# A gated graph layer whose loop gets a written order: logits in turn with sums, a fused product ahead of it, the next layer's weights in steps

## The chip, the cores and the metric

The kernel runs on one core of one Trainium2 chip. A core has engines that each run their own instruction stream: TensorE (matmuls into PSUM[...]; PE in the profile, its weight loads PEld), VectorE (DVE), ScalarE (ACT), GpSimd (POOL) and SyncE (SP), which here only issues DMAs. They wait for each other on semaphores. The metric is the device time of one execution in microseconds, and lower is better. Before the change the median of three runs is 1995.79 us (1994.71 to 1996.02).

## The reference

Four graph layers follow each other on a matrix x of 2708 nodes by 128 features, with one dense weighted adjacency matrix adj of 2708 by 2708; each layer's output is added to x, and x is normalised (`x = layernorm(x + layer(x, adj))`). The change is in the second one, called layer 1:

```
messages = x @ W_msg + b_msg
q = messages @ W_q;  k = messages @ W_k
probs = sigmoid(q @ k.T / sqrt(128) + gate_bias)
gates = probs * adj * adj                    # the prior is adj again
aggregated = gates @ messages
updated = relu(concatenate([x, aggregated]) @ W_upd + b_upd)
x = layernorm(x + layernorm(updated) * gamma + beta)
```

Layer 0 computes messages with a gelu for every pair of neighbours. Layer 2 is a layer in hyperbolic space; it has a weight W, a bias b and two attention vectors, and b needs some arithmetic of its own before use (its norm, a tanh, its products with the attention vectors). Layer 3 multiplies adj with x twice. All is f32.

## The kernel before

The 2708 nodes are 22 row tiles of 128, the last with 20 rows. x lies in SBUF for the whole kernel, one tile per 128 columns. The layers run one after the other in one program. The function `layers_1_to_3` (L959) begins with layer 1.

Its first stage goes over groups of up to four tiles: x is transposed (into xT), multiplied with W_msg (mT, the messages with features on partitions), then with the product of W_q and the transpose of W_k (qT), so that a logit is a product of qT and mT; `sums` (L258) makes the messages in rows (mrow) from xT and W_msg, one product of 128 columns per tile. A GpSimd addition (xb, L1003) prepares x plus beta.

The loop (L1012) goes over the 22 tiles of k. A tile of the transposed adjacency (2708 columns, 1354 KB) comes from HBM through SyncE's queue, with three buffers. The 2708 columns are five PSUM banks of 512 and one of 148. For each bank TensorE makes the logits (L1024) into one of two PSUM buffers called lg, and ScalarE puts their sigmoid into w (L1025). VectorE multiplies the whole row of w with the adjacency twice (L1027 and L1028, 128x2708 each); then six products (L1030) add it up, with mrow as weights, in one PSUM tile acc of six banks, over all 22 tiles. There are two w buffers. After the loop VectorE copies acc to aggT (L1032).

The update (L1041) then makes two products per tile, of xT with the upper half of W_upd and of aggT with the lower, adds the bias on VectorE, applies relu on ScalarE and takes the moments of every tile (`moments`, L197). `Resnorm` (L220) normalises twice in two halves of the tiles: `add` for both halves (normalise, times gamma, plus xb, new moments), then `end` for both.

The class `Weights2` (L290) prepares layer 2's weights: it loads W into w2 and the three vectors both as rows spread over all partitions (vecs, by GpSimd's queue, L299) and as columns (SyncE's queue), makes a transpose of W, the arithmetic on the bias, and three columns beside W. It is called at tiles 5, 11 and 16.

What sets the order: in this layer no order is written; a scheduler puts the instructions of each engine in a sequence by what it expects of their times and dependences. It does not have to keep the order of the program: it moved Weights2's loads and its first arithmetic to the very start of the layer, and layer 2's first adjacency loads (L1224) to its start, too. In layers 0 and 3, and in part of layer 2, the order is written: inside `tc.manual_schedule()` each engine runs its instructions as the program lists them.

Of the kernel before, what the change touches and what calls it, by code (L numbers as in the profile page):

```python
# [39 lines left out]
def gnn_stack(ctx: ExitStack, tc: tile.TileContext, t, out: bass.AP):  # L40
# [50 lines left out]
    def over_tiles(r, n=NT, p=P):  # L91
        return r[:p, None, :].to_broadcast([p, n, r.shape[1]])
# [8 lines left out]
    class Values:  # L101


        def __init__(self, pool, tag):
            self.pool, self.tag, self.n = pool, tag, 0
# [155 lines left out]
    def sums(dst, a, b, r, terms, psum, bias):  # L261

        ps = psum.tile([P, BANK // D, D], F32, name="ps")
        for i in range(a, b):
            for k, (src, w) in enumerate(terms):
                nc.tensor.matmul(ps[:r, i - a, :], src[:, i * P:i * P + r], w,  # L266
                                 start=k == 0, stop=k == len(terms) - 1)
        nc.vector.tensor_tensor(dst, ps[:r, :b - a, :], over_tiles(bias, b - a, r), op=ALU.add)  # L268
# [18 lines left out]
    y = const.tile([P, D], F32, name="y")  # L287
    yw = const.tile([P, 3], F32, name="yw")

    class Weights2:  # L290
        def __init__(self, pool):
            self.pool = pool

        def load(self):
            nc.sync.dma_start(out=w2[:, :D], in_=t["L2_WT"])
            self.vecs = self.pool.tile([P, 3, D], F32, name="y2_vecs")
            self.cols = self.pool.tile([P, 3], F32, name="y2_cols")
            for k, name in enumerate(("L2_gnn_b", "L2_gnn_att_wl", "L2_gnn_att_wr")):
                nc.gpsimd.dma_start(out=self.vecs[:, k, :], in_=t[name].partition_broadcast(P))  # L299
                nc.sync.dma_start(out=self.cols[:, k:k + 1], in_=t[name].rearrange("(p o) -> p o", o=1))  # L300
            self.w_rows = self.pool.tile([P, D], F32, name="y2_w_rows")
            self.prods = self.pool.tile([P, 3, D], F32, name="y2_prods")

        def products_with(self, dst, v):
            nc.vector.tensor_tensor(self.prods, self.vecs, v[:, None, :].to_broadcast([P, 3, D]), op=ALU.mult)
            nc.vector.tensor_reduce(dst, self.prods, AX.X, ALU.add)

        def turn(self, ps):
            nc.tensor.transpose(ps[:, :D], w2[:, :D], ident)
            nc.vector.tensor_copy(self.w_rows, ps[:, :D])  # L310

        def bias_point(self):
            V = Values(self.pool, "y2_")
            vecs, cols = self.vecs, self.cols
            sums3 = self.pool.tile([P, 3], F32, name="y2_sums")
            self.products_with(sums3, vecs[:, 0, :])
            bn = V.norm(sums3[:, 0:1])
            bth = V.act(bn, AF.Tanh)
            bk = V.mul(V.mul(bth, V.recip(bn)), V.shrink(bth))
            nc.vector.tensor_scalar(y, vecs[:, 0, :], bk, None, op0=ALU.mult)  # L320
            nc.vector.tensor_copy(vecs[:, 0, :], y)
            nc.vector.tensor_tensor(cols[:, 0:1], cols[:, 0:1], bk, op=ALU.mult)
            self.products_with(yw, y)

        def columns(self, ps):
            nc.tensor.matmul(ps[:, :3], self.w_rows, self.cols, start=True, stop=True)
            nc.vector.tensor_copy(w2[:, D:], ps[:, :3])

# [628 lines left out]
    def layers_1_to_3(top):  # L959

        with ExitStack() as l1:
# [3 lines left out]
            qT = wp.tile([P, N], F32, name="qT")  # L965
            mT = wp.tile([P, N], F32, name="mT")
            aggT = wp.tile([P, N], F32, name="aggT")
            mrow = wp.tile([P, NT, D], F32, name="mrow")
            xb = wp.tile([P, NT, D], F32, name="xb")
            w_msg, w_q, w_k = weight("L1_gnn_W_msg"), weight("L1_gnn_W_q"), weight("L1_gnn_W_k")  # L970
            upd_x, upd_a = weight("L1_gnn_W_upd", 0), weight("L1_gnn_W_upd", P)
# [3 lines left out]

            with ExitStack() as pre:
                psum = pre.enter_context(tc.tile_pool(name="ps_pre1", bufs=2, space=PSUM))

                wT = []
                for w in (w_q, w_k):  # L980
                    ps = psum.tile([P, BANK], F32, name="ps")
                    nc.tensor.transpose(ps[:, :P], w, ident)
                    wT.append(wp.tile([P, P], F32, name=f"wT{len(wT)}"))
                    nc.vector.tensor_copy(wT[-1], ps[:, :P])
                w_qk = wp.tile([P, P], F32, name="w_qk")
                ps = psum.tile([P, BANK], F32, name="ps")
                nc.tensor.matmul(ps[:, :P], wT[0], wT[1], start=True, stop=True)
                nc.vector.tensor_copy(w_qk, ps[:, :P])
                for a, b, r in groups():
                    c = slice(a * P, (b - 1) * P + r)  # L990
                    n = c.stop - c.start
                    ps = psum.tile([P, BANK], F32, name="ps")
                    for i in range(a, b):
                        nc.tensor.transpose(ps[:, (i - a) * P:(i - a) * P + r], x[:r, i, :], ident[:r, :r])
                    nc.scalar.copy(xT[:, c], ps[:, :n])
                    ps = psum.tile([P, BANK], F32, name="ps_m")
                    nc.tensor.matmul(ps[:, :n], w_msg, xT[:, c], start=True, stop=True)
                    nc.scalar.activation(mT[:, c], ps[:, :n], AF.Identity, bias=msg_bc)
                    ps = psum.tile([P, BANK], F32, name="ps_q")
                    nc.tensor.matmul(ps[:, :n], w_qk, mT[:, c], start=True, stop=True)  # L1000
                    nc.vector.tensor_copy(qT[:, c], ps[:, :n])
                    sums(mrow[:r, a:b, :], a, b, r, [(xT, w_msg)], psum, msg_br)
                nc.gpsimd.tensor_tensor(xb, x, over_tiles(beta), op=ALU.add)  # L1003

            with ExitStack() as att:
                gp = att.enter_context(tc.tile_pool(name="gates", bufs=2))
                pacc = att.enter_context(tc.tile_pool(name="ps_agg1", bufs=1, space=PSUM))
                plog = att.enter_context(tc.tile_pool(name="ps_log", bufs=2, space=PSUM))
                acc = pacc.tile([P, N], F32, name="acc")
                weights2 = Weights2(wp)  # L1010
                for j, r in enumerate(rows):
                    at = stream.tile([P, N], F32, name="at")  # L1012
                    nc.sync.dma_start(out=at[:r, :], in_=adjT[j * P:j * P + r, :])
                    if j == NT // 4:
                        weights2.load()
                    elif j == NT // 2:
                        weights2.turn(plog.tile([P, BANK], F32, name="lg"))
                        weights2.bias_point()
                    elif j == NT * 3 // 4:
                        weights2.columns(plog.tile([P, BANK], F32, name="lg"))  # L1020
                    w = gp.tile([P, N], F32, name="w")
                    for a, b in spans(0, N, BANK):
                        lg = plog.tile([P, BANK], F32, name="lg")
                        nc.tensor.matmul(lg[:r, :b - a], mT[:, j * P:j * P + r], qT[:, a:b], start=True, stop=True)  # L1024
                        nc.scalar.activation(w[:r, a:b], lg[:r, :b - a], AF.Sigmoid, bias=gate_b[:r, :],  # L1025
                                             scale=1.0 / math.sqrt(D))
                    nc.vector.tensor_mul(w[:r, :], w[:r, :], at[:r, :])  # L1027
                    nc.vector.tensor_mul(w[:r, :], w[:r, :], at[:r, :])  # L1028
                    for a, b in spans(0, N, BANK):
                        nc.tensor.matmul(acc[:, a:b], mrow[:r, j, :], w[:r, a:b], start=j == 0, stop=j == NT - 1)  # L1030
                for a, b in spans(0, N, BANK):
                    nc.vector.tensor_copy(aggT[:, a:b], acc[:, a:b])  # L1032

            with ExitStack() as upd:
                rp = upd.enter_context(tc.tile_pool(name="upd1", bufs=1))
                psum = upd.enter_context(tc.tile_pool(name="ps_upd1", bufs=4, space=PSUM))
                V = Values(rp, "v1_")
                h = rp.tile([P, NT, D], F32, name="h")
                st = rp.tile([P, NT, 6], F32, name="st")
                nc.vector.memset(h[:, NT - 1, :], 0.0)  # L1040
                for a, b, r in groups():  # L1041
                    g = h[:r, a:b, :]
                    sums(g, a, b, r, [(xT, upd_x), (aggT, upd_a)], psum, upd_b)
                    nc.scalar.activation(g, g, AF.Relu)
                    moments(st, h, a, b)
                Resnorm(h, xb, gamma, st, rp.tile([P, NT, 6], F32, name="st2"), V, xsq).all()

# [584 lines left out]
```

## Time and profile before

| | |
|---|---|
| median of 3 runs | 1995.79 us |
| the profiled execution, and its span | 1993.64 us, 1991.8 us |
| mean granted TensorE clock | 0.92 |
| busy shares TensorE, VectorE, ScalarE, GpSimd | 84%, 77%, 55%, 34% |
| layer 0 | up to about 931.7 us |
| layer 1, first stage | 931.9 to about 970 |
| layer 1, loop up to its last sum | to 1196.4 |
| copies and update, up to the last moment | to 1214.4 |
| both normalisations | to 1239.8 |
| layer 2, layer 3 | to the end |

The profile is one execution; its times are microseconds from the start of its span. "Busy" is the time in which an engine works on an instruction. A line of a timeline names the start, the duration, the engine, the program's line, the operation, what it writes and reads, and how often it ran there; in brackets stands how long the engine was idle before it, and what ended this. The clock is TensorE's: 1.00 is the full one. The shares of the whole span are means over stages with different limits, so the change has to be read from the stretch between 931.9 and about 1246.

### The profile page before, as it was taken

What the parts mean: (1) busy time and instruction counts of PE and PEld (TensorE: products, weight loads), DVE (VectorE), ACT (ScalarE), POOL (GpSimd) and SP (SyncE); (2) the same over time, 40 slices, a digit from 0 to 9 for tenths busy, and PEclk for the clock granted to TensorE, in tenths of its full rate; (3) what the DMA queues carried; (4) which work ended last, traced back from release to release, by engine and by line L of the source; (5) the groups of instructions that cost most, each with busy time, mean ns of one, the idle gap of its engine ahead of it and who ended that gap; (6) DMA issues with size and microseconds to landing.
All of it is one profiled execution on the core that took longest, in us unless ns stands there. A gap on an engine that the chain in (4) does not pass through costs nothing. (4 is left out here: it accounts for less than half of the span.)

```text
span 1991.8 us, 36394 instructions
## 1 busy us (share of the span) xinstructions
PE 1663.9 (84%) x14037; PEld 949.8 (48%) x14037; DVE 1526.7 (77%) x3500; ACT 1103.2 (55%) x1519; POOL 679.0 (34%) x429
## 2 busy tenths in 40 slices
PE   5899999999999999871999994689898983089995
PEld 4666666666666666550444334322232321044542
DVE  7899999999999999876564658699999997810105
ACT  3666676666666666542433323599998983300103
POOL 5677677677577677461000000021000350000000
PEclk9899999999999999995999996779998986589998
DMA  8666666666666676432243310022222217034330
GB/s 224 150 130 135 138 139 128 136 141 127 136 148 122 136 147 111 82 66 88 114 141 139 127 45 1 1 87 88 75 81 95 81 42 293 0 144 167 112 116 30
DMA packets 218359, 222.25 MB, mean 112 GB/s; under 512 B 28373, under 2 KB 204475, under 8 KB 211715
## 3 DMA queue, kind: packets, MB, share of 16 engines
q1 hardware_dynamic: 167038, 195.95, 32.4%
q0 software_dynamic: 51136, 23.88, 10.3%
q8 instruction: 112, 1.84, 0.4%
q14 instruction: 73, 0.59, 0.1%
HBM read 211.94 MB, written 7.83 MB: 110 GB/s over the span
## 5 line engine op out<-in xcount | busy, mean ns | idle before, releaser
L722 POOL DMA_INDIRECT far<-d_tab,ix x352 | 561.8, 1596 | 259.2 <-DVE W L823 112.8
L836 ACT ACTIVATE g<-sl 128x768 f32<-128x768 f32 x484 | 393.4, 813 | 257.9 <-PE sl L763 238.1
L758 PE MATMUL sl<-dA,S 124*128 124x153 f16 x4840 | 408.8, 232 | 10.3 <-DVE W L823 7.8
L758 PEld LDWEIGHTS <-S 124*128 124x128 f16 x4840 | 331.1, 98 | 80.2 <-issue 68.4
L774 PE MATMUL acc<-g,W 128*32 128x128 f32 x4840 | 206.0, 278 | 0.5 <-DVE W L823 0.5
L1227 POOL TENSOR_TENSOR at<-at,off 128x128 f32<-128x128 f32 (+1 forms) x22 | 70.3, 3213 | 336.0 <-DVE m L1256 171.4
L1543 PE MATMUL acc<-held,x 128*128 128x512 f32 (+1 forms) x240 | 99.5, 563 | 84.1 <-DVE x L218 84.1
L774 PEld LDWEIGHTS acc<-g,W 128*32 128x32 f32 x4840 | 140.9, 109 | 58.6 <-issue 54.6
L763 PE MATMUL sl<-s,same 50*128 50x384 f16 x968 | 162.0, 308 | 0.0
L268 DVE TENSOR_TENSOR g<-ps,row_L_gnn_b 128x512 f32<-128x512 f32 (+2 forms) x14 | 7.9, 573 | 197.0 <-PE ps L266 196.9
L1025 ACT ACTIVATE w<-lg,row_L_gnn_gate_bias 128x512 f32<-128x512 f32 (+1 forms) x132 | 80.8, 635 | 137.7 <-PE lg L1024 74.3
L1283 PE MATMUL accV<-m,X 128*128 128x512 f32 (+4 forms) x264 | 128.4, 628 | 33.6 <-DVE m L1273 29.2
L823 DVE TENSOR_TENSOR W<-sl,own 128x150 f32<-128x150 f32 x484 | 143.3, 300 | 14.3 <-ACT g L836 13.6
L1235 PE MATMUL ps<-XT 128*128 128x512 f32 (+4 forms) x264 | 143.2, 626 | 3.1 <-ACT m L1240 2.8
L648 DVE TENSOR_SCALAR S<-rk 124x1000 f16<-124x1000 bf16 (+1 forms) x330 | 134.0, 431 | 0.0
L718 DVE FIND_INDEX8 ix<-v,o 128x8 uint32<-128x2728 f32 x44 | 131.7, 2994 | 0.0
L1024 PE MATMUL lg<-qT,mT 128*128 128x512 f32 (+2 forms) x264 | 115.6, 567 | 18.6 <-ACT w L1025 9.9
L1027 DVE TENSOR_TENSOR w<-w,at 128x2708 f32<-128x2708 f32 (+1 forms) x22 | 65.5, 2975 | 79.3 <-ACT w L1025 79.3
L736 DVE SCALAR_TENSOR_TENSOR extra<-far,v,extra 128x128 f32<-128x128 f32 x330 | 115.0, 349 | 6.3
L1543 PE MATMUL acc<-at,x 128*128 128x512 f32 (+3 forms) x288 | 116.8, 552 | 0.0
L680 DVE SCALAR_TENSOR_TENSOR o<-ps,ar 128x496 f32<-128x496 f32 x132 | 82.4, 624 | 37.3 <-PE ps L669 30.0
L1502 ACT COPY nT<-acc 128x512 f32<-128x512 f32 (+1 forms) x12 | 6.4, 531 | 186.5 <-PE acc L1543 186.5
(319 smaller groups left out, 2675.7 us busy)
## 6 DMA issues: line engine op xcount, KB each, us to landing
at<-in_adjT SPq DMA_DIRECT2D x40, 1354.0 KB
ar<-in_adj SPq DMA_DIRECT2D x105, 248.0 KB
far<-s_tab SPq DMA_DIRECT2D x44, 512.0 KB
at<-in_adjT SPq DMA_DIRECT2D x42, 448.0 KB
at<-in_adjT SPq DMA_DIRECT2D x21, 704.0 KB
at<-in_adjT SPq DMA_DIRECT2D x21, 650.0 KB
held<-in_adjT SPq DMA_DIRECT2D x10, 1354.0 KB
at<-in_adjT SPq DMA_DIRECT2D x21, 280.0 KB
```

The costliest lines, as they stand in the source:

```text
L648: nc.vector.tensor_scalar(self.S[h][:, :n, :, k * RG:(k + 1) * RG], self.rk[h][:, :n, :LR].rearrange("p b (c i) -> p b c i", c=NC), EDGE + ...
L718: nc.vector.max_index(ix, self.v[:, n * 8:n * 8 + 8], self.o.rearrange("p b j -> p (b j)"))
L722: nc.gpsimd.indirect_dma_start(out=self.far[n][:, k, :], out_offset=None, in_=d_tab[:, :], in_offset=bass.IndirectOffsetOnAxis(ap=self.ix[ ...
L758: nc.tensor.matmul(group[c], self.S[h][:, n, c, :], dA[q][:, b, c, :], start=c % 3 == 0 and q == 0, stop=False)
L763: nc.tensor.matmul(out, same[p], self.s3[p, :e - a, :], start=False, stop=True)
L774: nc.tensor.matmul(self.acc[q:q + 32, k, :], W[:, c, :], g[:, c, :], start=b == 0 and k == 0, stop=ends)
L823: nc.vector.tensor_tensor(W[:, :, :RG].rearrange("p (k c) i -> p k c i", k=2), columns_of(sl, D, DA), own[:, None, None, :].to_broadcast([ ...
L836: nc.scalar.activation(g.rearrange("p (k c) d -> p k c d", k=2), columns_of(sl, 0, D), AF.Gelu, scale=1.0 / D_SCALE)
L1024: nc.tensor.matmul(lg[:r, :b - a], mT[:, j * P:j * P + r], qT[:, a:b], start=True, stop=True)
L1235: nc.tensor.matmul(ps, XT[:, self.js], XT[:, c], start=True, stop=False)
L1283: nc.tensor.matmul(accV[:, a:b], X[:self.r, self.j, :], self.m[:, a:b], start=first, stop=last)
L1543: nc.tensor.matmul(acc[k], src[:rows[j], j, :], at[:rows[j], a:b], start=j == order[0], stop=j == order[-1])
```

## The change

It has three parts.

First, in the first stage, W_msg and the upper half of W_upd stand side by side in one tile w_both, and the two biases in b_both (four GpSimd copies). One product of 256 columns per tile makes the message row and the x half of the update, and both go to SBUF in one tile called both, of which mrow and h are the halves. The update after the loop then only needs the products with aggT, which are added to h.

Second, the loop, the update and `norm.all()` stand in `tc.manual_schedule()`. The adjacency is loaded two tiles ahead. For each bank there is a logits product, a sigmoid, two multiplications of that bank alone (264 of 128x512 or 128x148 in place of 44 of 128x2708), and then a product that adds up the same bank of an earlier tile: one tile back for the first seven tiles, two for the next seven, three for the others. Tiles 0, 7 and 14 therefore have logits only. The last three tiles are added up bank by bank; ScalarE copies each bank to aggT, and the update of a bank follows after the sums of the next, its moments one bank later. acc is six tiles of one bank, and there are four w buffers.

Third, Weights2 becomes a generator weights2 in steps; one step is taken at the end of each tile from tile 2. All its loads are on SyncE's queue, between those of tiles 4 and 5; the transpose, the norm, Sqrt, Tanh and the columns come at tiles 4 to 9.

```diff
-            nc.sync.dma_start(out=w2[:, :D], in_=t["L2_WT"])
...
-                nc.gpsimd.dma_start(out=self.vecs[:, k, :], in_=t[name].partition_broadcast(P))
-                nc.sync.dma_start(out=self.cols[:, k:k + 1], in_=t[name].rearrange("(p o) -> p o", o=1))
...
+        nc.sync.dma_start(out=w2[:, :D], in_=t["L2_WT"])
+        for k, name in enumerate(names):
+            nc.sync.dma_start(out=vecs[:, k, :], in_=t[name].partition_broadcast(P))
+            nc.sync.dma_start(out=cols[:, k:k + 1], in_=t[name].rearrange("(p o) -> p o", o=1))
+        yield
+        yield
+        ps = bank()
+        nc.tensor.transpose(ps[:, :D], w2[:, :D], ident)
...
+        s = V.act(sq, AF.Sqrt)
+        yield
...
+        bth = V.act(bn, AF.Tanh)
+        yield
...
-                    sums(mrow[:r, a:b, :], a, b, r, [(xT, w_msg)], psum, msg_br)
+                    for i in range(a, b, 2):
+                        m = min(i + 2, b)
+                        ps = psum.tile([P, 2, 2 * D], F32, name="ps_w")
+                        for k in range(i, m):
+                            nc.tensor.matmul(ps[:r, k - i, :], xT[:, k * P:k * P + r], w_both, start=True, stop=True)
+                        nc.vector.tensor_tensor(both[:r, i:m, :], ps[:r, :m - i, :], over_tiles(b_both, m - i, r),
+                                                op=ALU.add)
...
-                    nc.vector.tensor_mul(w[:r, :], w[:r, :], at[:r, :])
-                    nc.vector.tensor_mul(w[:r, :], w[:r, :], at[:r, :])
-                    for a, b in spans(0, N, BANK):
-                        nc.tensor.matmul(acc[:, a:b], mrow[:r, j, :], w[:r, a:b], start=j == 0, stop=j == NT - 1)
-                for a, b in spans(0, N, BANK):
-                    nc.vector.tensor_copy(aggT[:, a:b], acc[:, a:b])
...
+                def gates(j, k):
+
+                    r, (a, b) = rows[j], banks[k]
+                    if k == 0:
+                        ws[j] = gp.tile([P, N], F32, name="w")
+                    w, at = ws[j][:r, a:b], ats[j][:r, a:b]
+                    lg = plog.tile([P, BANK], F32, name="lg")[:r, :b - a]
+                    nc.tensor.matmul(lg, mT[:, j * P:j * P + r], qT[:, a:b], start=True, stop=True)
+                    nc.scalar.activation(w, lg, AF.Sigmoid, bias=gate_b[:r, :], scale=1.0 / math.sqrt(D))
+                    nc.vector.tensor_mul(w, w, at)
+                    nc.vector.tensor_mul(w, w, at)
+
+                def add_up(j, k):
+                    a, b = banks[k]
+                    nc.tensor.matmul(acc[k], mrow[:rows[j], j, :], ws[j][:rows[j], a:b], start=j == 0, stop=j == NT - 1)
...
+                def update(k):
+                    for a, b, r in of_bank(k):
+                        ps = plog.tile([P, BANK], F32, name="lg")[:r].rearrange("p (i d) -> p i d", d=D)
+                        for i in range(a, b):
+                            nc.tensor.matmul(ps[:, i - a, :], aggT[:, i * P:i * P + r], upd_a, start=True, stop=True)
+                        g = h[:r, a:b, :]
+                        nc.vector.tensor_tensor(g, g, ps[:, :b - a, :], op=ALU.add)
+                        nc.scalar.activation(g, g, AF.Relu)
...
+                with tc.manual_schedule():
+                    load(0)
+                    load(1)
+                    summed = 0
+                    for j in range(NT):
+                        if j + 2 < NT:
+                            load(j + 2)
+                        lag = 1 if j < NT // 3 else 2 if j < NT * 2 // 3 else LAST
+                        for k in range(len(banks)):
+                            gates(j, k)
+                            if j - summed >= lag:
+                                add_up(summed, k)
+                        summed += j - summed >= lag
+                        if j > 1:
+                            next(made, None)
+                    for k, (a, b) in enumerate(banks):
+                        for j in range(summed, NT):
+                            add_up(j, k)
+                        nc.scalar.copy(aggT[:, a:b], acc[k])
+                        if k > 0:
+                            update(k - 1)
+                        if k > 1:
+                            look(k - 2)
+                    update(len(banks) - 1)
+                    look(len(banks) - 2)
+                    look(len(banks) - 1)
+                    norm.all()
```

## The prediction, made before the changed kernel had run

> **What bounds the kernel now.** I read the page first, then busy time and clock in stretches of layer 1, then TensorE's timeline in its loop, then the waits. The page gives a span of 1991.8 us; the profiled execution took 1993.64, against a median of 1995.79. Everything that the diff touches lies between 931.9 us (layer 1 starts) and 1246.0 (layer 2's first own operation), so I cost that stretch. First the stretches; columns: window, its length, busy time of each engine with its instructions, granted TensorE clock, DMA share, GB/s.
>
> ```profile
> span 1991.8 us, 36394 instructions
> core 0: us, PE busy (x) PEld busy (x) DVE busy (x) ACT busy (x) POOL busy (x), PEclk, DMA share, GB/s
> 931.00:949.00 18.00, 7.74 (x27) 5.07 (x28) 3.48 (x10) 1.86 (x3) 7.81 (x4) 0.69 0.80 281
> 1040.00:1080.00 40.00, 37.90 (x95) 16.07 (x94) 22.43 (x9) 14.64 (x24) 0.00 (x0) 1.00 0.37 136
> 1191.00:1196.00 5.00, 5.00 (x9) 2.01 (x7) 0.00 (x0) 0.00 (x0) 0.00 (x0) 0.51 0.00 0
> 1215.00:1236.00 21.00, 0.74 (x4) 0.76 (x5) 20.65 (x90) 4.86 (x14) 2.39 (x8) 0.50 0.00 0
> ```
>
> The loop is bound by TensorE (37.90 of 40 us, full clock) with VectorE at 56%, so only its 5% of gaps can be won. Before the loop TensorE is busy 7.74 of 18; the loop ends at half clock; behind it VectorE alone works (20.65 of 21). TensorE's timeline (start, us, lines, count, idle before with its releaser) shows the gaps:
>
> ```profile
> 1040.07 9.49 PE L1030 MATMUL acc<-w,mrow 128*128 128x512 f32 x24
> 1049.40 3.18 PE L1024 MATMUL lg<-qT,mT 128*128 128x512 f32 x8
> 1053.10 5.19 PE L1024 MATMUL lg<-qT,mT 128*128 128x512 f32 x12 [0.53 <-ACT w L1025]
> 1058.81 1.98 PE L1024 MATMUL lg<-qT,mT 128*128 128x512 f32 x4 [0.52 <-ACT w L1025]
> 1060.63 9.48 PE L1030 MATMUL acc<-w,mrow 128*128 128x512 f32 x24
> ...
> 1183.14 4.81 PE L1030 MATMUL acc<-w,mrow 128*128 128x512 f32 x12 [1.41 <-DVE w L1028]
> 1189.02 7.35 PE L1030 MATMUL acc<-w,mrow 20*128 20x512 f32 x12 [1.07 <-DVE w L1028]
> ```
>
> The scheduler had formed pairs of tiles: 9.33 us of sums for two (1040.07 to 1049.40), then 11.2 us of logits, 20.56 per pair, 10.28 per tile. Twelve products of a tile cost 9.33 back to back; logits in a row run at the pace of two PSUM buffers that ScalarE empties. The third gap is at the start:
>
> ```profile
> 947.44 0.56 DVE L305 TENSOR_TENSOR y_prods<-y_vecs 128x384 f32<-128x384 f32 x1 [7.80 <-DMA y_vecs<-in_L_gnn_att_wr]
> 948.65 2.08 PE L1024 MATMUL lg<-qT,mT 128*128 128x512 f32 x2 [8.45 <-DVE qT L1001]
> ```
>
> VectorE stood 7.80 us at layer 2's vectors, which the scheduler had put ahead of layer 1's own qT copies, and TensorE 8.45 us behind it.
>
> [...] the trace has 691 (L1566). [...] here a load itself takes 1.283. [...] L811 has a mean of 774 for the same 128x512 add, up to 1.14 us while GpSimd's L813 ran.
>
> **The change, part by part.**
>
> Before the loop. The five groups of four tiles ran at 4.14 us each once steady (TensorE's timeline has ps_m at 954.41, 958.55, 962.69), with one bank of the first tile's logits (.86) inside each. After, the messages' 22 products are 256 columns wide instead of 128, four at .21 more a group, and the logits leave: 4.2 a group. With layer 2's vectors gone from the front, I put the first group at 935.3, cold, 5.3 us; four at 4.2 = 16.9; the last two groups, of one tile each, 3.0: 960.5. Then tile 0's six logits come alone, 5.4, after the sigmoid table's 1.3: tile 1 starts at 967.2 against 970.2. **−3.0.** Bounds: −8 (cold part shorter) to +3. The five small GpSimd operations for the joined weights stand ahead of xb (6.1 us) and only the third is awaited by a matmul of the first group; they are hidden under 3 us of transposes.
>
> The loop. Tiles 1 to 21: 19 with both kinds of product at 9.33, and two (7 and 14, where the lag grows) with logits alone at 5.4: 177.3 + 10.8 = 188.1. Layer 2's steps cost about 1.5 in all: two table loads around Sqrt (1.28 each; ScalarE is busy some 3.8 of 9.33, so about .4 shows), and two small products that take a logits buffer until VectorE has emptied it, .9. Tanh needs no load, by the order of the instructions. 189.6. Then 18 banks of sums remain, 3 × 4.665 = 13.9 by bank sizes. Before, from 970.2 to the last sum at 1196.4 was 226.2; after 203.5: **−22.7**, of which about 20 is the 5% and the rest the cold last sums. VectorE's bill grows: 44 multiplies of 128x2708 (2.98, 5.95 a tile) become 264, ten of .691[...], each with the .035 that lies between two neighbours now: 7.95 a tile, under 9.33. Queued behind a multiply are only later multiplies, and the sums that need one are a tile or more behind. On SP's queue the adjacency runs two tiles ahead: 1.39 MB in 9.33 us is 149 GB/s, with 281 shown at the start. Seven loads for layer 2 pass ahead of one tile's (.31 to .49 us issue each, 3 us), hidden by those two tiles.
>
> The end. Before: last sum 1196.4, copies on VectorE to 1199.7, 88 update matmuls to 1212.5, moments to 1214.4: 18.0. After: half of these matmuls is already done, copies and updates run between the banks; 22 × 2 × .107 = 4.7 of TensorE's time remains and about 1.9 behind it for the last add, relu and two moments: 6.6. **−11.4.** Layer 3 ends in the same pattern and shows that it holds at full rate (chain of waits: one bank's three sums, 2.58, then its eight small products):
>
> ```profile
> 1850.87 2.58 PE acc L1543 x6
> 1853.45 0.89 PE ps L266 x8
> ```
>
> The normalise. It is now in written order on VectorE, each half's short operations one after another; before, the scheduler interleaved two halves, 31.6 us from the last moment (1214.4) to layer 2's first (1246.0). In layer 0, in written order, the two adds took 10.35 (the second; 12.4 with a table load) and the two ends 4.8 and 4.5; so 10.6 + 10.35 + 6.0 with layer 2's memset and offsets inside, .6 and two of 5.3 for its early norm: 38.2. **+6.6**, from +2 to +9.
>
> Layer 2's first adjacency tiles (four of 704 KB) were asked for at 935.8 and will now be asked for when the normalise ends. Their first reader began 54.8 us after that end at 1239.9; 2.8 MB at 280 GB/s is 10. Hidden; without that cover it would cost those 10.
>
> Sum: −3.0 − 22.7 − 11.4 + 6.6 = −30.5 on 1993.64, 1963.1. The median lies 2.15 over the profiled execution: 1965.
>
> **Rivals.**
> (a) The alternation does not pack. A logits product now always follows a sum, each with a wait on another engine; .06 us lost at each of 228 pairs makes a tile 10.0: 19 × .67 = 12.7 given back, 1978. For it: every product waits by itself. Against: the logits at 1049.40 follow the sums without a gap, and layer 3's bank order is 100% busy. The clock belongs here: the last tile has 20 rows, and its sums at half clock in the last three tiles would cost up to 7.
> (b) More than I count: the group before the loop warms sooner, layer 3's 4.55 a tile holds in place of 4.665 (−5), and the normalise overlaps better (+2): 1952.
> (c) Slower: VectorE becomes the bound. It needs more than .83 us a 128x512 multiply to pass 9.33 a tile; at .914 a tile is 10.18 and over 22 tiles all 30.5 us are gone; at L811's 1.14 a tile is 12.4, 2015. For it: L811. Against: [...] it does nothing in the loop after xb, near tile 0; VectorE's sequence of waits could do it too, but none longer than .035 shows between neighbours.
> (d) Nothing changes: the scheduler's loop was as full as it can be and only the end wins, then paid to the normalise. The 5% of gaps speaks against it: 1993 to 1998.
>
> **How the numbers follow.** My case (1958 to 1974) .70, (a) .14, (b) .06, (c) .06, (d) .04. Leaving out two in ten would allow 1956 to 1980; I keep 1953 to 1982 since the half-clock stretches are not known to a few us. 0.2% (4 us) is about what a measurement of this kernel can tell from none. Faster: my case, (a) and (b): .90. Slower: (c) and a little of (d): .07. Same .03.
>
> **What would show it.** Sums and logits in turn, one tile every 9.3 us, TensorE over 98% in the loop, multiplies at .69 with VectorE near 85%; no wait of VectorE at layer 2's vectors, and tile 1 near 967; last sum near 1171, last moment near 1177; 36 to 40 us from there to layer 2's first norm; no wait for layer 2's adjacency. I am wrong if multiplies exceed .83, if TensorE waits for SP's or VectorE's semaphores every bank, or if the end runs at half clock.

## The result: 1964.8 us, and where the time went

Four runs of the changed kernel have a median of 1964.78 us (1962.89 to 1965.96), against 1995.88 for the kernel before, run four times beside it; the ratio is 0.9847, with a 95% interval of 0.9835 to 0.9859. The profiled execution took 1964.59 us. The page's span, and the busy times by stretch (window, its length, busy time of each engine with its instructions, granted TensorE clock, DMA share, GB/s):

```profile
span 1962.8 us, 36538 instructions
core 0: us, PE busy (x) PEld busy (x) DVE busy (x) ACT busy (x) POOL busy (x), PEclk, DMA share, GB/s
970.00:1000.00 30.00, 30.00 (x80) 14.21 (x79) 25.91 (x44) 12.58 (x20) 0.00 (x0) 1.00 0.49 161
1100.00:1145.00 45.00, 45.00 (x119) 21.08 (x118) 36.87 (x61) 19.02 (x30) 0.00 (x0) 1.00 0.28 98
1150.00:1170.00 20.00, 20.00 (x57) 7.29 (x56) 7.44 (x15) 5.44 (x10) 0.00 (x0) 1.00 0.00 1
1180.00:1210.00 30.00, 5.27 (x23) 4.94 (x24) 26.81 (x109) 6.60 (x17) 0.71 (x4) 0.50 0.00 1
```

In these stretches of the loop and of its bank-by-bank end TensorE has no gap left, at full clock. What gaps remain are small: 0.53 us at ScalarE behind each of the two later tiles with logits alone (tiles 7 and 14), 0.31 us at one of layer 2's steps, and 0.56 us at the last update. The normalise behind it keeps VectorE busy and TensorE mostly idle, as before. TensorE's timeline after the change shows the turn of products (an f32 product counts as two instructions, so x2 is one), one per 0.86 us with the next always ready:

```profile
976.41 1.02 PE L1058 MATMUL acc<-w,both 128*128 128x512 f32 x2
977.27 0.41 PE L1051 MATMUL lg<-qT,mT 128*128 128x148 f32 x2
977.52 0.41 PE L1058 MATMUL acc<-w,both 128*128 128x148 f32 x2
977.78 1.02 PE L1051 MATMUL lg<-qT,mT 128*128 128x512 f32 x2
978.63 1.02 PE L1058 MATMUL acc<-w,both 128*128 128x512 f32 x2
...
986.86 1.02 PE L1051 MATMUL lg<-qT,mT 128*128 128x512 f32 x2
```

From 977.78 to 986.86 is one tile: 9.08 us, where it was 10.28.

Layer 0, the same in all kernels here, ended 2.4 us later in this execution (in the runs below layer 1 starts between 931.5 and 934.2), so I count layer 1 from its own start, the transpose of W_q on TensorE (931.90 before, 934.33 after), up to layer 2's first value on VectorE:

| us from layer 1's start | before | after | difference of the stretch |
|---|---|---|---|
| tile 1 starts | 38.3 | 34.3 | -4.0 |
| last moment of the update | 282.5 | 245.6 | -32.9 |
| layer 2's first value | 314.1 | 283.4 | +6.2 |
| from there to the end of the span | 745.8 | 745.1 | -0.7 |

Layer 1 is 30.7 us shorter.

### The profile page after: what moved, and what is told of

Same layout as the page of the kernel before. It is cut to its first block, busy times and chain, and to the rows that moved or that the text cites. A ratio compares the mean times of both kernels' runs of the same rounds, so it can differ in the third digit from the quotient of the medians.

```text
span 1962.8 us, 36538 instructions
## 1 busy us (share of the span) xinstructions
PE 1652.3 (84%) x13993; PEld 948.7 (48%) x13993; DVE 1561.3 (80%) x3718; ACT 1111.1 (57%) x1527; POOL 679.2 (35%) x431
## 3 DMA queue, kind: packets, MB, share of 16 engines
q1 hardware_dynamic: 167470, 196.15, 32.9%
## 5 line engine op out<-in xcount | busy, mean ns | idle before, releaser
L1051 PE MATMUL lg<-qT,mT 128*128 128x512 f32 (+2 forms) x264 | 121.1, 547 | 3.6 <-ACT w L1052 3.1
L1058 PE MATMUL acc<-w,both 128*128 128x512 f32 (+2 forms) x264 | 121.2, 547 | 0.0
```

What stands on the lines that cost most here:

```text
L1058: nc.tensor.matmul(acc[k], mrow[:rows[j], j, :], ws[j][:rows[j], a:b], start=j == 0, stop=j == NT - 1)
```

## The experiments

In what follows "layer 1" is this count, 283.4 for the changed kernel and 314.1 for the one before. A ratio compares a run with runs of the kernel before that were taken beside it, whose medians lie between 1993.48 and 1995.23; in brackets behind it stands its 95% interval. So where a time and a ratio differ by a few us, the ratio is the better comparison.

**The normalise alone left to the scheduler.**

```diff
                     look(len(banks) - 1)
-                    norm.all()
+                norm.all()
```

> The changed kernel with the normalise alone left to the scheduler again. My theory: the written order makes VectorE run two chains of short dependent operations one after the other, which costs 6.2 us (37.8 us from the last moment of the update to layer 2's first value on VectorE, against 31.6 before the change). So this stretch falls to 31 to 33 us and the time to about 1959. The rival: the stretch is longer for another reason (what layer 2 puts into it, or its data arriving otherwise), and the scheduler's order gives nothing: 37 to 38 us, 1965.

Measured: 1958.66 us, ratio 0.9819 (0.9802 to 0.9835). From VectorE's timeline, the last moments of the update (start, duration) and layer 2's first value, in the changed kernel:

```profile
1178.73 1.24 DVE L197 BATCH_NORM_STATS2 st<-both 128x6 f32<-128x128 f32 x6
...
1217.75 0.16 DVE L140 TENSOR_SCALAR w<-xsq 128x22 f32<-128x22 f32 x1
```

The same lines of VectorE's timeline with the normalise free:

```profile
1178.55 1.24 DVE L197 BATCH_NORM_STATS2 st<-both 128x6 f32<-128x128 f32 x6
...
1211.40 0.16 DVE L140 TENSOR_SCALAR w<-xsq 128x22 f32<-128x22 f32 x1
```

37.8 us have become 31.6, and layer 1 is 278.0. The written order of the normalise is a cost of 6 us that the change need not have paid.

**The kernel before with its normalise in written order**, the same edit from the other side.

```diff
-                Resnorm(h, xb, gamma, st, rp.tile([P, NT, 6], F32, name="st2"), V, xsq).all()
+                last = Resnorm(h, xb, gamma, st, rp.tile([P, NT, 6], F32, name="st2"), V, xsq)
+                with tc.manual_schedule():
+                    last.all()
```

> The kernel before, with only its normalise in written order. My theory: 6 us more, 37 to 38 us in the stretch from the last moment to layer 2's first value against 31.6, 2002. The rival: no change, 1996, which would mean that the longer stretch after the change comes from elsewhere.

Measured: 1998.33 us, ratio 1.0015 (1.0008 to 1.0022), so about 3 us more, where I had expected 2002. The stretch went from 31.6 to 36.9, layer 1 from 314.1 to 318.7. The direction is as expected, the size of the stretch nearly; the time shows less than the stretch.

**Rows in turn: six logits, then six sums.**

```diff
                         for k in range(len(banks)):
                             gates(j, k)
+                        for k in range(len(banks)):
                             if j - summed >= lag:
                                 add_up(summed, k)
```

> The changed kernel, but in each tile all six banks of logits come before all six sums, in the same written order otherwise. My theory: the gain in the loop is the alternation, since logits in a row wait for ScalarE to empty two PSUM buffers. A tile then takes 4.55 of sums and 5.4 to 5.6 of logits, 10.0 to 10.2 against 9.09, and the kernel 18 to 21 us more: 1983 to 1986. The rival: what gained is the written order with loads two tiles ahead and multiplies by bank, whatever the turn of the products: within 4 us of 1965.

Measured: 1969.06 us, ratio 0.9867 (0.985 to 0.9883), 4.3 us above the changed kernel; layer 1 is 290.3. My number fell: a tile takes 9.46, not 10.0. TensorE's timeline, weight loads among it (PEld), has the reason:

```profile
978.64 5.08 PE L1051 MATMUL lg<-qT,mT 128*128 128x512 f32 x12
979.07 0.19 PEld L1051 LDWEIGHTS lg<-qT,mT 128*128 128x128 f32 x1 [0.24 <-issue]
979.50 0.19 PEld L1051 LDWEIGHTS lg<-qT,mT 128*128 128x128 f32 x1 [0.24 <-issue]
980.44 0.30 PEld L1051 LDWEIGHTS lg<-qT,mT 128*128 128x128 f32 x2 [0.75 <-ACT w L1052]
981.30 0.30 PEld L1051 LDWEIGHTS lg<-qT,mT 128*128 128x128 f32 x2 [0.56 <-ACT w L1052]
982.34 0.30 PEld L1051 LDWEIGHTS lg<-qT,mT 128*128 128x128 f32 x2 [0.75 <-ACT w L1052]
...
983.56 4.71 PE L1058 MATMUL acc<-w,both 128*128 128x512 f32 x12
988.10 1.45 PE L1051 MATMUL lg<-qT,mT 128*128 128x512 f32 x3
```

The first two logits of a row find both PSUM buffers empty, since ScalarE emptied them during the sums. Only from the third on does a load wait for ScalarE, and then two banks take 1.90 us (980.44 to 982.34) instead of 1.72. A row of six loses 0.37 (4.92 from 978.64 to 983.56), and what follows the short bank is a sum, which needs no buffer. So of the 1.2 us per tile that the loop gained, 0.37 came from the alternation itself, and 0.8 with the rest of the written order: 0.7 of it in the logits (5.6 a tile in the scheduler's pairs, 4.92 here), 0.1 in the sums. I take the long rows of the pairs for its cause; that the multiplies by bank and the two more w buffers had no part in it is not shown. I had given all of it to the alternation.

**The kernel before, with even banks.** What costs the time in a long row: the width, or the short bank?

```diff
+                even = list(enumerate(spans(0, N, 452)))
...
-                    for a, b in spans(0, N, BANK):
+                    for _, (a, b) in even:
```

The sums and the copies behind the loop take the same banks.

> The kernel before, with the 2708 columns of its loop cut into five banks of 452 and one of 448 in place of five of 512 and one of 148; order, products and work are the same. My theory, after the run with whole rows in turn: the lost time of the loop before is not the pace of ScalarE (.86 of product against .69 of sigmoid for each full bank) but sits behind the short bank, whose product takes .25 us while the sigmoid of the bank ahead of it still holds the buffer that is needed next; about 1.07 us for each tile. Even banks take it away: a pair of tiles falls from 20.56 to between 18.4 and 19.2 us, and the kernel to 1973 to 1983. The rival: two buffers are too few for logits in a row at any width[...]: the pair stays above 20, the time within 4 us of 1995.

Measured: 1991.82 us, ratio 0.999 (0.9981 to 0.9998): at most 4 us, not the 12 to 22 of my theory. The rival holds. TensorE's timeline in this run:

```profile
1045.71 4.71 PE L1031 MATMUL acc<-w,mrow 128*128 128x452 f32 x12
1050.25 9.67 PE L1025 MATMUL lg<-qT,mT 128*128 128x452 f32 x22
1059.76 4.73 PE L1031 MATMUL acc<-w,mrow 128*128 128x452 f32 x12
1065.26 1.03 PE L1025 MATMUL lg<-qT,mT 128*128 128x452 f32 x2 [0.78 <-ACT w L1026]
1066.12 4.71 PE L1031 MATMUL acc<-w,mrow 128*128 128x452 f32 x12
```

A pair of tiles still takes 20.41 (1045.71 to 1066.12). The visible gaps at the short bank are gone, but eleven logits take 9.51 (1050.25 to 1059.76) where eleven products of 0.757 are 8.33. The two runs fit one account of a long row: a buffer comes round once in a product, a sigmoid and about 0.35 us in which neither works on it (what fills these no run shows): .86 + .69 + .35 = 1.90 for 512 columns, .76 + .64 + .35 = 1.75 for 452, both as measured. With two buffers that is one bank per 0.95 or 0.87 us, always above the product. The prediction's reading of the row of logits, paced by two buffers that ScalarE empties, fits after all; the alternation removes the wait because a sum stands between two logits. A run with a third buffer, which would test this directly, was not made.

**The kernel before, without layer 2's vectors at the front.**

```diff
-            self.vecs = self.pool.tile([P, 3, D], F32, name="y2_vecs")
-            self.cols = self.pool.tile([P, 3], F32, name="y2_cols")
+            late = self.late()
+            self.vecs = late[:, :3 * D].rearrange("p (k d) -> p k d", d=D)
+            self.cols = late[:, 3 * D:3 * D + 3]
...
+                weights2.late = lambda: stream.tile([P, N], F32, name="at")
```

All steps of Weights2 then come at tile 5.

> The kernel before, with layer 2's vectors loaded into one of the adjacency's buffers in the middle of the loop, so that the scheduler cannot take them to the front of the layer. My theory: the 7.8 us wait of VectorE at the front goes, and tile 1 starts 4 to 8 us sooner counted from the layer's start; the loop has one disturbed tile (0 to 3 us). Time 1988 to 1994. The rival: the front is bound by TensorE's half clock and its products, the wait lies beside them: tile 1 at 38 us as before, time 1996 or a little more.

Measured: 2002.68 us, ratio 1.0043 (1.0029 to 1.0057), slower, and layer 1 is 323.3. As a forecast of the time it fell, but the front answers the question. The stretch of logits that started at 969.95 before starts here at 962.28, with the layer's start at 934.01: 28.3 us instead of 38.1. The vectors' loads and arithmetic at the front cost 9.8, more than my 4 to 8. All of it is lost again before the update ends, and 8 us more (the last moment comes at 290.5, against 282.5): VectorE waits 5.47 us for the same vectors, and the loop ends with an idle TensorE. VectorE's timeline in this run, at the first of the steps:

```profile
1001.39 0.56 DVE L306 TENSOR_TENSOR y_prods<-at 128x384 f32<-128x384 f32 x1 [5.47 <-DMA at<-in_L_gnn_att_wr]
```

TensorE's timeline in the same run, at the last sums of the loop:

```profile
1197.96 9.39 PE L1030 MATMUL acc<-w,mrow 20*128 20x512 f32 x12 [6.78 <-DVE w L1028]
```

So layer 2's vectors cost where they are waited for. How much of the loop's loss is this wait is not shown: in this run the vectors also take one of the adjacency's three buffers.

**All of layer 2's steps at once**, at the end of tile 4.

```diff
-                        if j > 1:
+                        if j == 2:
                             next(made, None)
+                        if j == 4:
+                            for _ in made:
+                                pass
```

> The changed kernel with all of layer 2's arithmetic done at the end of tile 4 in place of one step for each tile. My theory: at once, VectorE stands in its chain until ScalarE has come to the Sqrt and the Tanh behind its sigmoids and table loads, and the sums of the tile behind run out of finished rows while lag is one tile: 2 to 5 us lost, 1967 to 1970. The rival: VectorE has more room than that (a tile needs 7.3 us of it in this kernel's trace, of 9.09), and takes the lost time back within two tiles: less than 1 us in the loop.

Measured: 1971.33 us, ratio 0.9884 (0.9869 to 0.9899); layer 1 is 291.1, 7.7 more, above my range. TensorE's timeline, and VectorE's last work on the columns ahead of it:

```profile
1010.97 0.15 DVE L325 TENSOR_TENSOR y_cols<-y_cols,y 128x1 f32<-128x1 f32 x1
1011.22 0.56 PE L331 MATMUL lg<-y_cols,y_w_rows 128*128 128x3 f32 x2 [5.79 <-issue]
```

The cause is not the one I gave. TensorE did not run out of rows; it stood for 5.79 us in its own order at the product of the columns. The profile names no releaser, but by the program this product needs the columns that VectorE ends at 1011.12, and that chain holds two turns of ScalarE, the second behind a table load of 1.28 (in the changed kernel the Tanh at 1029.99 comes behind sigmoids, and the trace has no load before it). The clock over 1000 to 1050 was 0.93, against 1.00 in the changed kernel. The edit of the change that I priced at 1.5 us, "in steps", is worth some 7 against all of it at one place.

**The fused product undone.**

```diff
-                            nc.tensor.matmul(ps[:r, k - i, :], xT[:, k * P:k * P + r], w_both, start=True, stop=True)
...
+                    sums(mrow[:r, a:b, :], a, b, r, [(xT, w_msg)], psum, msg_br)
...
+                            nc.tensor.matmul(ps[:, i - a, :], xT[:, i * P:i * P + r], upd_x, start=True, stop=False)
-                            nc.tensor.matmul(ps[:, i - a, :], aggT[:, i * P:i * P + r], upd_a, start=True, stop=True)
+                            nc.tensor.matmul(ps[:, i - a, :], aggT[:, i * P:i * P + r], upd_a, start=False, stop=True)
```

> The changed kernel with the fused product undone: messages alone before the loop (128 columns), and both products of the update behind it. My theory: the 22 products of 128 columns are only moved from one stretch that TensorE bounds to another, so the front is 4 us shorter, the end 4 to 5 longer, and the time within 1.5 us of 1965. The rival: at the front these products lie under other work (ScalarE's and VectorE's copies), so undoing them gives nothing there and the end pays in full: 1968 to 1970.

Measured: 1961.81 us, ratio 0.9841 (0.9824 to 0.9859), which the intervals do not part from the changed kernel; layer 1 is 282.1, 1.3 less. The first sum comes 5.1 us sooner (30.1 from the layer's start, against 35.2) and the last moment 0.7 sooner. The front gains more than the products, because tile 0's logits lie among the groups again:

```profile
954.30 0.60 PE L1002 MATMUL ps<-ident,x 128*128 128x128 f32 x4
954.74 1.02 PE L1040 MATMUL lg<-qT,mT 128*128 128x512 f32 x2
955.60 1.10 PE L1005 MATMUL ps_m<-xT,w_L_gnn_W_msg 128*128 128x512 f32 x2
```

The fused form has a fourth PSUM tile by name in the first stage. With two buffers each these are eight banks by the program, where three names make six; the loop has eight of its own (six of acc, two of lg). That tile 0's logits wait for buffers of that stage is a guess of mine, which no run shows. What the traces show is their place: the first of them starts at 942.62 here, 8.6 us after the layer's start, and at 961.55 in the changed kernel, 27.2 after it.

**The tile of 20 rows first.**

```diff
+                turn = [NT - 1] + list(range(NT - 1))
```

Loads, gates and sums take turn[j] in place of j.

> The changed kernel with the tile of 20 rows taken first instead of last; all else as it is. In the changed kernel's trace a pair of products takes 2.02 us instead of 1.72 where one of them has only 20 rows, and the last three sums of a bank take 2.86 instead of 2.58. My theory: going back and forth between a product of 20 rows and one of 128 costs .1 to .2 us each time; first in the loop its logits stand alone, and the last banks have full tiles only: 1.5 to 3 us less, 1962 to 1963.5, with 2.6 us for three sums of a bank at the end. The rival: the end is slower for another reason (clock, or copies and updates between the banks): 2.86 stays, 1965.

Measured: 1965.22 us with a wide spread (1959.22 to 1968.53), ratio 0.9861 (0.984 to 0.9882): no verdict on the time. Layer 1 is 282.2, 1.2 less, a little under my range. On the cause the trace speaks; the end of the loop on TensorE in the changed kernel:

```profile
1163.15 2.93 PE L1058 MATMUL acc<-w,both 128*128 128x512 f32 x6
1166.01 1.16 PE L1068 MATMUL lg<-w_L_gnn_W_upd,aggT 128*128 128x128 f32 x8
1167.01 2.93 PE L1058 MATMUL acc<-w,both 128*128 128x512 f32 x6
```

The same place on TensorE's timeline with the short tile first:

```profile
1163.83 2.74 PE L1063 MATMUL acc<-w,both 128*128 128x512 f32 x6
1166.40 1.05 PE L1073 MATMUL lg<-w_L_gnn_W_upd,aggT 128*128 128x128 f32 x8
1167.30 2.74 PE L1063 MATMUL acc<-w,both 128*128 128x512 f32 x6
```

Three sums and eight small products take 3.86 with a 20-row product among them, 3.47 without, at full clock in both. The theory holds for the end; the first sum starts 1.3 us later, which takes part of it back.

**Four more multiplies for each tile on VectorE.**

```diff
+                idle = rp.tile([P, BANK], F32, name="idle")
...
+                    if k < 4:
+                        nc.vector.tensor_mul(idle[:r, :b - a], w, at)
```

> The changed kernel with four more multiplies of 128x512 per tile on VectorE, into a tile that nobody reads. My theory, the prediction's: VectorE is at 7.95 us of the 9.09 that a tile takes on TensorE, so it becomes the bound as soon as 1.1 us are added; with 4 x .727 a tile takes 10.8 to 10.9 and the kernel 35 to 40 us more, 2000 to 2005, slower than before. The rival: VectorE's real room is larger, because sums run up to three tiles behind and TensorE's waits hide it: less than 15 us more.

Measured: 1992.91 us, ratio 0.9994 (0.9985 to 1.0002): 28 us more than the changed kernel, where I had 35 to 40. By the ratio, whose interval holds 1, the whole gain is gone. VectorE is the bound: at the end TensorE waits for it,

```profile
1174.71 1.12 PE L1061 MATMUL acc<-w,both 128*128 128x512 f32 x2 [2.71 <-DVE w L1055]
1184.79 6.81 PE L1061 MATMUL acc<-w,both 20*128 20x512 f32 x8 [8.96 <-DVE w L1055]
```

and a tile of multiplies took 10.11 us of VectorE in the middle of the loop (1102.46 to 1112.57). The size was off since a bank costs VectorE less than I counted. Its timeline in the changed kernel, just behind a step of layer 2 where it is catching up:

```profile
1051.01 0.68 DVE L1053 TENSOR_TENSOR w<-w,at 128x512 f32<-128x512 f32 x1
1051.72 0.69 DVE L1054 TENSOR_TENSOR w<-w,at 128x512 f32<-128x512 f32 x1
1052.33 0.69 DVE L1053 TENSOR_TENSOR w<-w,at 128x512 f32<-128x512 f32 x1
1053.06 0.69 DVE L1054 TENSOR_TENSOR w<-w,at 128x512 f32<-128x512 f32 x1
```

The second multiply, which needs the first, starts 0.71 after it; the next bank's, which needs neither, starts 0.61 after that, before it has ended. A bank is 1.32 to 1.33, not 1.45; five of them and a short one of 0.57 are about 7.2 us a tile, where the prediction had 7.95.

**The sums one tile behind all along.**

```diff
-                        lag = 1 if j < NT // 3 else 2 if j < NT * 2 // 3 else LAST
+                        lag = 1
```

> The changed kernel with the sums one tile behind from the first tile to the last. Two tiles of logits alone (7 and 14, 6.57 us each where their six products need 4.55) go, and only the 20-row tile is left to be added up bank by bank. My theory: the rows of one tile back are ready in time as they are now for the first seven tiles, so the loop keeps 9.09 a tile; the growing lag only fills the end with sums while copies and updates run, and without it TensorE waits there for ScalarE's copies and VectorE's adds: 2 to 4 us gained in the loop and 2 to 6 lost at the end, the time within 3 us of 1965. The rival: a lag of one is too short, single tiles wait for VectorE and the loop loses 5 us or more.

Measured: 1962.42 us (1958.5 to 1966.49), ratio 0.9846 (0.9831 to 0.9861): not to be told from the changed kernel. Layer 1 is 282.0, 1.4 less. The growing lag is not what gains. Nor does the loss at the end that I expected show: there TensorE waits once, 0.21 us. (The 6.57 us in my expectation for tiles 7 and 14 includes the next tile's first bank; tile 14 alone, from 1085.18 to 1090.79, is 5.61.)

**Two edits together: unfused, and the normalise free.**

> Two earlier edits together: the fused product undone, and the normalise left to the scheduler. My theory: they act in different stretches and add up, 1.3 us by the first (layer 1 counted from its start to layer 2's first value) and 6.2 by the second: layer 1 at 276, the time at 1956 to 1958, ahead of both kernels. The rival: the gain of the first was chance, 1958 to 1960, as with the normalise alone.

Measured: 1955.3 us (1953.4 to 1958.21), ratio 0.9807 (0.9794 to 0.9821). It beats both kernels: the interval lies below the changed kernel's, 0.9835 to 0.9859. Layer 1 is 277.0, against 278.0 with the normalise alone, so of the first edit's 1.3 us about 1.0 shows; that part is as small as the differences between runs.

**The first half's normalise ahead of the last updates**, on top of that.

```diff
                         if k > 1:
                             look(k - 2)
+                        if k == 4:
+                            norm.add(0, NT // 2)
...
-                norm.all()
+                norm.add(NT // 2, NT)
+                for a, b in runs():
+                    norm.end(a, b)
```

> As the kernel with the product unfused and the normalise left to the scheduler, but the first half's normalise stands in the written order ahead of the last two banks' updates, since its tiles (0 to 10) are complete by then. My theory: VectorE is idle for 2.4 to 3.2 us of each 3.9 at the end of layer 1, and what it does of the first half there is off the end: 2 to 4 us, layer 1 at 272 to 274. The rival: the last banks' updates queue behind 10 us of normalise on VectorE, TensorE stands and its clock falls, and what is won is given back: 275 to 278.

Measured: 1959.92 us, ratio 0.9835 (0.9821 to 0.9848), 4.6 more than without it. The rival holds: the updates queue behind the normalise, TensorE stands for them, and its clock over 1176 to 1186 is 0.57,

```profile
1183.77 0.61 PE L1057 MATMUL lg<-w_L_gnn_W_upd,xT 128*20 128x128 f32 x2 [6.47 <-DVE both L1060]
```

so that the last moment comes 9.6 us later and the rest of the normalise is 9.2 shorter: layer 1 is 277.4. The rest of the loss lies in layer 2, which was 4.5 us longer in this profile; why is open.

## Why the prediction was right, by its steps

The time was forecast as 1965 and came out as 1964.8; that this is so near is partly luck, since errors of both signs met.

**Before the loop, -3.0; measured -4.0.** The first stage ended 27.2 us after the layer's start against my 28.6, and tile 0's logits took 7.0 against 6.7. The forecast was near because two effects met whose sizes I had not seen: the vectors at the front were worth 9.8, and the fused product and the exposed logits of tile 0 took back nearly 6 of it.

**The loop and the end, -34.1; measured -32.9.** Three terms were mis-sized. A tile takes 9.09, not 9.33: rival (b) had named layer 3's 4.55 per six products, and it holds here; over 19 tiles this gives 4.6. Tiles 7 and 14 took 5.6 each, not 5.4, and the 20-row tile's logits, alternating with full sums, 10.5. The whole from tile 1 to the last logits was 187.4 against 189.6. From there to the last moment it was 24.0 against my 13.9 + 4.7 + 1.9 = 20.5, and this term was too small by 3.5: the 20-row product among the last sums costs about 0.4 a bank. In the run with that tile first the same stretch takes 21.6 (1157.54 to 1179.09), so 2.4 of the 3.5 belong to the short tile; the last 1.1 is not accounted for, and holds the 0.56 at the last update. The clock, which I had put beside rival (a) with up to 7 us, stayed at 1.00.

**Why the loop gained.** The sum was right, the sharing was not: the run with whole rows in turn shows 0.37 us of the 1.2 per tile from the alternation and 0.8 from the rest of the written order, its shorter rows by my reading.

**VectorE's bill, 7.95 a tile; measured about 7.2**, so its room was larger than I said. The tile at which I had the gain end, 10.18, fits the run with four more multiplies, 10.11. But .914 per multiply was too near: as its neighbours overlap, I estimate .99 for such a tile (five banks of two multiplies less .06, and .57). Rival (c) also had a wrong sum: 12.4 a tile is 2.2 over that break-even, 49 us over 22 tiles, which makes about 2044 of 1995, not 2015. That VectorE can become the bound is real, as four more multiplies show, but nothing in the loop came close. The 1.14 that I took from L811 is one of its five adds of 128x512 in layer 0: it starts at 894.33, while GpSimd's L813 runs (893.65 to 894.91), and the other four take 0.68 to 0.69; whether L813 delayed it no run shows. What stands against (c) is that GpSimd's busy time in the loop is 0.00 (1040 to 1080 before the change, 1000 to 1145 after). The 7.95 includes two multiplies of 128x148 a tile: a line through the 2.98 us at 2708 columns and 0.691 at 512 of the kernel before gives, as an estimate, 0.312 for one, and the changed kernel's means are 0.305 and 0.312.

**Layer 2's steps, 1.5; measured about 2.** This is what is left of the 187.4 when tiles at 9.09, the two at 5.6 and the 20-row tile are taken off. The cover is the spreading over tiles: without it the cost is 7.7.

**The normalise, +6.6; measured +6.2**, and confirmed from both sides.

**Layer 2's adjacency** was asked for at 1212.38, as forecast, and the rest of the kernel is 0.7 us shorter, not longer: hidden.

Rival (a), alternation that packs badly, is refuted by a tile of 9.08 with no gap; (d) by the same.

One reading does not hold as it stands. I took the half clock before the change, at 1191, for a consequence of 1.41 and 1.07 us of idle time. But the full sums right behind the 1.41 ran at full rate (six in 4.81), and in layer 3 the same fall comes without idle time. TensorE's timeline there, in the kernel before:

```profile
1747.85 10.84 PE L1543 MATMUL acc<-held,x 128*128 128x512 f32 x24 [84.09 <-DVE x L218]
1758.62 6.93 PE L1543 MATMUL acc<-at,x 20*128 20x512 f32 x12
1765.48 7.73 PE L1543 MATMUL acc<-held,x 128*128 128x512 f32 x12
1773.05 4.71 PE L1543 MATMUL acc<-at,x 128*128 128x512 f32 x12
```

The clock was 1.00 from 1753.62 to 1758.62. Then six sums of 20 rows followed without a gap; from 1762.48 on it was 0.50, and the six full sums behind them took 7.73 where 4.71 is usual. Layer 3 shows this in 13 of the 14 traces of this case (in the changed kernel 7.68 for the six full sums, behind a clock of 0.50); in the run with the short tile first the same 20-row sums took 4.80 at 1.00, and why is open. So half clock came here with no idle time just before it: the 84 us of idle time lie further back, and full clock stood between. The six 20-row sums are what precedes the fall in layer 3, but no run takes them away there, and whether idle time had a part at 1191 is not shown. After the change the last 20-row tile of layer 1 stands among full products, and the clock stays at 1.00.

## What to carry to other kernels

Where one engine refills what another empties through two buffers, put work between that needs no buffer: here a row of six cost 0.37 us a tile over the alternation, and a long one ran at a product, an evacuation and 0.35 us for every two banks. In this kernel a written order paid where one engine is the bound and its partners are each a step behind; it cost 6 us where the work is two chains of short dependent operations, which the scheduler interleaves, so look for that border and end the written region there. Side work with a chain over several engines cost its waits in the place where it is issued: spread it one link at a time, and look where a fused product leaves the next stage's first work: here tile 0's logits began 27.2 us after the layer's start, against 8.6 unfused, and the first sum came 5.1 us later.

## What the runs showed of the hardware that I had not expected

At full clock a product with weights or rows of 20 next to one of 128 cost extra: a pair of 512-column products took 2.02 us with 20-row logits (1145.51 to 1147.53 in the changed kernel) against 1.72, and three sums with eight small products 3.86 against 3.47. On VectorE an f32 multiply of 128x512 took 0.69 us, but one that did not need its predecessor started 0.61 after it, one that did 0.71 to 0.73. The way of a PSUM buffer from product to sigmoid and back held about 0.35 us in which neither engine worked on it, by estimate from the 1.90 us for 512 columns and the 1.75 for 452. And the clock fell from 1.00 to 0.50 within six 20-row sums in a row, with TensorE at work for the 11 us before them, in 13 of 14 traces; in layer 1 of the changed kernel, with these sums among full products, it did not fall.
